# Attention scores on 32-row tiles of TensorE, four tiles at a time, in a transformer and state-space block on one Trainium2 core

## The chip, the cores and the metric

The kernel runs on one core of a Trainium2 chip. The metric is the device time of one execution in microseconds. TensorE multiplies matrices (PE in the profile, its weight loads PEld), VectorE is DVE, ScalarE is ACT, GpSimd is POOL, and SyncE (SP) issues transfers.

## The reference

Two layers work on x of shape (4, 256, 512). Layer 0 adds an attention and a gated feed-forward network, both of the normalized x; layer 1 adds a selective scan and a mixture of experts. What matters here is layer 0's attention:

```python
C_q = x @ Wq_d + bq_d                                   # 12 numbers per token
C_kv = x @ Wkv_d + bkv_d                                # 4 numbers per token
q = (C_q @ W_qk + b_qk).reshape(b, s, 32, 4)            # 32 heads of 4
scores = jnp.einsum('bqhd,bkd->bhqk', q, C_kv) / jnp.sqrt(4)
attn = jax.nn.softmax(scores, axis=-1)
V = (C_kv @ Wv_u + bv_u).reshape(b, s, 32, 16)
out = jnp.einsum('bhqk,bkhd->bqhd', attn, V).reshape(b, s, 512)
return out @ Wo + bo
```

All heads share the keys C_kv, and a head's contraction has length 4. The feed-forward network runs beside it: `silu(x @ W_gate.T) * (x @ W_up.T) @ W_down.T` with an inner width of 1792.

## The kernel before, in words

The order of the work is written out by hand (`tc.manual_schedule()`); each engine executes its instructions in the order of the program text. Layer 0 takes batches 0 and 1 as a first half and batches 2 and 3 as a second.

**Latents.** `latents(b)` (L269) makes the queries and keys of batch b, as a generator whose steps are put between other work. An fp32 value is held as two fp32r parts, high and low, each in four rows of a group of eight (for keys: two high copies, one low part and ones). `pkm` (L289) multiplies the keys `ks` with the selection `selk`; there are four selections, one for each position h4 = 0..3 of a head in its group of four, and each leaves the rows of the other three heads at zero. The result `km` has 128 rows and four versions, of 256 keys each. The queries `qg` have 128 rows too: 4 heads of 32 rows, for 4 groups gq and 2 halves hf, so 32 heads.

**Maxima.** `scores_max(b, j)` (L324) makes scores with queries on the partitions: for one gq, hf and query block qb, two matmuls (L329) of all 128 rows of `qg` with two versions of `km` each, 512 columns, into one PSUM tile `sc` of 1024 columns; zeros in `km` pick the head. VectorE then reduces it to four maxima (L331). Sixteen calls make a batch. `put_max(b)` (L336) transposes the maxima and adds them into rows of `qg` with eight VectorE instructions (L348), so that the next product is already score minus maximum.

**Attention.** `attention(b, ff, after, first, step, side)` (L467) runs eight steps k, one for each pair of key block c and head position h4. In each, `attend(b, k, t)` for t = 0, 1 makes transposed scores (keys on the partitions) with two matmuls `scT` (L361) of 128 rows, 512 columns, and ScalarE takes exp of 1024 columns (L363) into `pe`. `weigh(b, k-1)` (L365) sums the values `zk` with the weights of the step before: four matmuls of 32 output columns each, on four column tiles (fp32, so eight passes, L371). If `after` holds, which is so for b = 0 and 2, each step also has two calls of `scores_max` for batch b+1, one on each side of `weigh`. The maxima of batches 0 and 2 are made ahead, each in a loop of its own (L525, L552), together with `second`, the latents of the next batch. `normalize` (L375) copies the sums, multiplies them with a matrix that repeats the denominators (`pden`, L380), and VectorE divides.

`sc` and `scT` share the pool `pssc`, which has two slots of two PSUM banks. Other matmul results go to `psmm`, three slots of one bank.

**Feed-forward beside it.** `ff` is a generator: `gate_up(th)` (L403) makes, for 14 chunks, a gate (`pg`) and an up product (`pu`) of eight matmuls each of 512 columns (L417), and yields after every two; ScalarE takes tanh, VectorE multiplies (L425, L427), ScalarE rounds (L428), GpSimd makes the low part (L429) and issues the loads of weights `wgu` three products ahead. That is 112 pieces for each half. `go(ff, n)` runs n of them. `step` says how many pieces a step of attention takes, and `first` how many run behind `put_max`. After the first half, `down(0, i)` is the generator in place of `gate_up`.

After layer 0, pools are closed and layer 1 starts: projections, then a scan of 128 steps on VectorE (L909), with decays on ScalarE (L888), products on GpSimd (L913) and sums on TensorE (L925).

Of the kernel before, what the change touches and what calls it, by code (L numbers as in the profile page):

```python
# [17 lines left out]
P = 128  # L18
B, S, D = 4, 256, 512
# [22 lines left out]
def block_kernel(  # L42
# [24 lines left out]
    nc = tc.nc  # L67
    mm = nc.tensor.matmul
# [15 lines left out]
    ident = cst[:, C_ID : C_ID + P]  # L84
# [8 lines left out]
    psmm = ctx.enter_context(tc.tile_pool(name="psmm", bufs=3, space=PSUM))  # L93
# [8 lines left out]
    ap1 = att.enter_context(tc.tile_pool(name="att", bufs=1, side="right"))  # L102
# [18 lines left out]
    make = fold.enter_context(tc.tile_pool(name="fold", bufs=1))  # L121
# [4 lines left out]
    zq = make.tile([P, 4, 4 + P], F32, name="zq")  # L126
    nc.gpsimd.memset(zq, 0.0)

    zs = make.tile([40, 4, P], F32, name="zs")
    nc.gpsimd.memset(zs, 0.0)  # L130
    zz = make.tile([40, S], F32, name="zz")
    nc.gpsimd.memset(zz, 0.0)
    selq = ap1.tile([P, 4, 4 + P], F32R, name="selq")
    selk = ap1.tile([40, 4, P], F32R, name="selk")
    ks = ap1.tile([40, S], F32R, name="ks")
    mask = ap1.tile([P, 8], F32, name="mask")

# [9 lines left out]
    def selections():  # L147
        zh = zq[:, :, 4:].rearrange("p g (h r) -> p g h r", h=4)
        for r in (0, 8):
            nc.gpsimd.tensor_copy(zh[:, :, :, r : r + 4], idh[:, :, :, 0:4])  # L150
        nc.gpsimd.tensor_copy(selq, zq)
        for h4 in range(4):
            for k in range(2):
                nc.gpsimd.tensor_copy(
                    zs[32 * k : 32 * k + 8, h4, 32 * h4 + 8 * k : 32 * h4 + 8 * k + 8].rearrange(
                        "p (a r) -> p a r", a=2
                    ),
                    ident[32 * k : 32 * k + 8, 32 * k : 32 * k + 4].unsqueeze(1)
                    .to_broadcast([8, 2, 4]),
                )  # L160
            nc.gpsimd.tensor_copy(
                zs[0:8, h4, 32 * h4 + 16 : 32 * h4 + 24], ident[0:8, 4:5].to_broadcast([8, 8])
            )
        nc.gpsimd.tensor_copy(selk, zs)
        nc.gpsimd.tensor_copy(ks, zz)
# [101 lines left out]
    qs, kms = {}, {}  # L267

    def latents(b):  # L269
# [12 lines left out]
        yield  # L282
        yield

        km = ap1.tile([P, 4, S], F32R, tag="km", name="km", bufs=2)
        for h in range(2):
            p = psmm.tile([P, 2, S], F32, tag="mm", name="pkm")
            for i in range(2):
                mm(p[:, i, :], lhsT=selk[:, 2 * h + i, :], rhs=ks, start=True, stop=True)  # L289
            (nc.scalar.copy if h else nc.vector.tensor_copy)(km[:, 2 * h : 2 * h + 2, :], p)  # L290
        kms[b] = km
        yield
        pq = psmm.tile([P, 2, S], F32, tag="mm", name="pq")
        q8 = ap1.tile([P, 2, S], F32, tag="q8", name="q8")
        for hf in range(2):
            mm(pq[:, hf, :], lhsT=wqk[:, 1 + hf * P : 1 + (hf + 1) * P], rhs=cq,
               start=True, stop=True)
# [17 lines left out]
        for gq in range(4):  # L315
            p = psmm.tile([P, 2, S], F32, tag="mm", name="pqg")
# [4 lines left out]
            (nc.scalar.copy if gq % 2 else nc.vector.tensor_copy)(qg[:, gq], p)  # L321
            yield

    def scores_max(b, j):  # L324

        gq, hf, qb = j // 4, j // 2 % 2, j % 2
        sc = pssc.tile([P, 2, 512], F32, tag="sc", name="sc")
        for hp in range(2):
            mm(sc[:, hp, :], lhsT=qs[b][:, gq, hf, qb * P : (qb + 1) * P],  # L329
               rhs=kms[b][:, 2 * hp : 2 * hp + 2, :], start=True, stop=True)  # L330
        nc.vector.tensor_reduce(  # L331
            mpl2[b % 2][:, qb, :, 16 + 2 * gq + hf].rearrange("p (a i) -> p a i", a=2),
            sc.rearrange("p a (i k) -> p a i k", i=2), AX.X, ALU.max,
        )

    def put_max(b):  # L336
# [15 lines left out]
    avs, pes = {}, {}  # L352

    def attend(b, k, t):

        c, h4 = k // 4, k % 4
        if t == 0:
            pes[b, k] = ap1.tile([P, 4, 512], F32, tag="pe", name="pe", bufs=2)
        sc = pssc.tile([P, 2, 512], F32, tag="sc", name="scT")
        for j in range(2):  # L360
            mm(sc[:, j, :], lhsT=kms[b][:, h4, c * P : (c + 1) * P], rhs=qs[b][:, 2 * t + j],  # L361
               start=True, stop=True)
        nc.scalar.activation(pes[b, k][:, 2 * t : 2 * t + 2, :], sc, AF.Exp)  # L363

    def weigh(b, k):  # L365

        c, h4 = k // 4, k % 4
        if k == 0:
            avs[b] = psav.tile([P, 2, S], F32, tag="av", name="av")
        for gq in range(4):  # L370
            mm(avs[b][32 * gq : 32 * gq + 32].rearrange("p a b -> p (a b)"),  # L371
               lhsT=zk[:, 2 * b + c, 24 - 8 * h4 : 56 - 8 * h4], rhs=pes[b, k][:, gq, :],
               start=(c == 0 and h4 == 0), stop=(c == 1 and h4 == 3))

    def normalize(b, ff):  # L375
# [80 lines left out]
    def go(gen, n=1000):  # L456
        for _ in range(n):
            if next(gen, 1) == 1:
                break
# [7 lines left out]
    def attention(b, ff, after, first, step, side=()):  # L467

        put_max(b)
        go(ff, first)  # L470
        side = list(side)
        for k in range(8):
            attend(b, k, 0)
            go(ff, 1)
            attend(b, k, 1)
            go(ff, 1)
            if after:
                scores_max(b + 1, 2 * k)
            if k:
                weigh(b, k - 1)  # L480
            if after:
                scores_max(b + 1, 2 * k + 1)
            go(ff, step - 2)
            if side:
                f, *args = side.pop(0)
                f(*args)
        go(ff, 1)
        weigh(b, 7)
        go(ff, 1)
        normalize(b, ff)  # L490
# [28 lines left out]
    ff = gate_up(0)  # L519
    masks()  # L520
    first, second = latents(0), latents(1)
    for _ in range(9):
        go(first, 1)
        go(ff, 1)
    for j in range(16):  # L525
        scores_max(0, j)
        if j in (4, 8):
            fold_att(j // 8)
            go(ff, 1)
        else:  # L530
            go(ff, 2 if j % 3 else 1)
        if j % 2 == 1:
            go(second, 1)
    go(second)
    attention(0, ff, True, 8, 4)
    attention(1, ff, False, 8, 2, [(ln_begin, 1)] + [(ln_stats, 1, i) for i in range(4)]
              + [(ln_root, 1, 0, 4), (ln_scale, 1, 0, 2)])
    go(ff)
# [10 lines left out]
    for _ in range(9):  # L549
        go(first, 1)  # L550
        go(ff, 1)
    for j in range(16):  # L552
        scores_max(2, j)
        go(ff, 2)
        if j % 2 == 1:
            go(second, 1)
    go(second)
    go(ff)
    hidden(1)
    ff = gate_up(1)  # L560
    attention(2, ff, True, 10, 4)
# [700 lines left out]
    for u in range(total + 2):  # L1262
# [8 lines left out]
        if last >= 0 and last % NU == NU - 1:  # L1271
            c = last % PER // NU
# [124 lines left out]
```

## Time and profile before

| what | value |
|---|---|
| median of three runs | 887.26 us (887.15 to 890.01) |
| the profiled execution's own time | 889.37 us |
| its span, first to last instruction | 887.6 us |
| mean granted clock of TensorE | 0.927 |
| TensorE, VectorE, ScalarE, GpSimd busy | 85%, 77%, 59%, 55% |
| maxima of batch 0 | 29.0 to 60.3 us |
| attention of batches 0 and 1 | 60.3 to 110.3 and 110.3 to 148 us |
| maxima of batch 2 | 177.4 to 211 us |
| attention of batches 2 and 3 | 211 to 261.5 and 261.5 to 307 us |
| all after that | 307 to 888 us |

The stages are cut where `put_max` and `normalize` of a batch stand in the trace. A matmul of 512 columns has a duration of about 0.39 us in the records, while the next one starts 0.23 us after it: the records include the time to flow through, so prices are taken from differences of starts. fp32 matmuls count as two passes. A busy share of TensorE therefore says whether something is in flight, not how well it is used.

### The profile page before, as it was taken

What the parts mean: (1) busy time and instruction counts of PE and PEld (TensorE: products, weight loads), DVE (VectorE), ACT (ScalarE), POOL (GpSimd) and SP (SyncE); (2) the same over time, 40 slices, a digit from 0 to 9 for tenths busy, and PEclk for the clock granted to TensorE, in tenths of its full rate; (3) what the DMA queues carried; (4) which work ended last, traced back from release to release, by engine and by line L of the source; (5) the groups of instructions that cost most, each with busy time, mean ns of one, the idle gap of its engine ahead of it and who ended that gap; (6) DMA issues with size and microseconds to landing.
All of it is one profiled execution on the core that took longest, in us unless ns stands there. A gap on an engine that the chain in (4) does not pass through costs nothing.

```text
span 887.6 us, 10460 instructions
## 1 busy us (share of the span) xinstructions
PE 756.4 (85%) x3554; PEld 434.2 (49%) x3554; DVE 685.2 (77%) x675; ACT 525.8 (59%) x1009; POOL 489.9 (55%) x377
## 2 busy tenths in 40 slices
PE   5999989999989999998687898668898777965966
PEld 3675555667556576665453444334454433422422
DVE  4695554377565333878999999999999999999995
ACT  4225445312536437678787687776786794855561
POOL 4222222001223242758967789869689759697664
PEclk9999999899999999978997999888999889989896
DMA  6232242001112231374741645341646232426200
GB/s 213 60 95 72 72 119 71 13 1 36 48 48 72 72 116 26 96 185 153 239 111 51 165 120 159 98 127 54 166 134 163 84 96 75 126 72 178 72 24 24
DMA packets 67343, 86.67 MB, mean 98 GB/s; under 512 B 12077, under 2 KB 52025, under 8 KB 66906
## 3 DMA queue, kind: packets, MB, share of 16 engines
q1 hardware_dynamic: 57930, 67.12, 27.0%
q0 software_dynamic: 9072, 18.35, 7.5%
q8 instruction: 28, 0.46, 0.2%
q10 hardware_dynamic: 288, 0.52, 0.2%
q14 instruction: 25, 0.20, 0.1%
HBM read 66.58 MB, written 10.22 MB: 87 GB/s over the span
## 4 chain that ended last, share of the span: by engine, by line
DVE 39%; PE 36%; ACT 11%; POOL 6%; issue 5%; DMA 2%; SPq 0%; DVEq 0%; ACTq 0%; POOLq 0%
DVE h L909 23%; DVE bx L894 8%; ACT decay L888 5%; PE pu L417 5%; PE pg L417 4%; POOL hc L913 4%; PE sc L329 4%; PE av L371 3%; PE po L442 3%; PE scT L361 3%; PE px L696 2%; PE po L1017 2%; ACT pe L363 1%; PE ysum L925 1%; PE pqg L319 1%
## 5 line engine op out<-in xcount | busy, mean ns | idle before, releaser
L913 POOL TENSOR_TENSOR hc<-h,cr 128x1024 f32<-128x1024 f32 (+1 forms) x131 | 301.9, 2307 | 100.6 <-DVE h L909 89.1
L909 DVE TENSOR_TENSOR_SCAN h<-decay,bx 128x1024 f32<-128x1024 f32 (+1 forms) x129 | 288.0, 2234 | 15.6 <-PE po L442 3.9
L888 ACT ACTIVATE decay<-dts,aneg 128x255 f32<-128x255 f32 x504 | 213.6, 498 | 121.0 <-DVE h L909 110.6
L925 PE MATMUL ysum<-hc,stack 128*32 128x256 f32 x1024 | 93.0, 432 | 83.8 <-POOL hc L913 83.6
L894 DVE TENSOR_TENSOR bx<-brow,dus 128x1024 f32<-128x1024 f32 x128 | 157.6, 1231 | 3.7
L429 POOL TENSOR_TENSOR hlo<-g,hhi 128x512 fp32r<-128x512 f32 x28 | 36.1, 1290 | 148.5 <-ACT hhi L428 148.5
L331 DVE TENSOR_REDUCE mpl<-sc 128x4 f32<-128x1024 f32 x64 | 77.2, 1222 | 24.1 <-PE sc L329 23.8
L925 PEld LDWEIGHTS ysum<-hc,stack 128*32 128x32 f32 x1024 | 21.8, 113 | 146.0 <-POOL hc L913 125.5
L400 POOL DMA_DIRECT2D wgu<-in_wgu x56 | 31.2, 557 | 92.7 <-PE pg L417 82.4
L363 ACT ACTIVATE pe<-scT 128x1024 f32<-128x1024 f32 x64 | 62.7, 1023 | 29.9 <-PE scT L361 29.6
L1017 PE MATMUL po<-ow,xc 128*128 128x512 f32 x128 | 73.2, 682 | 2.2 <-DVE xc L929 2.2
L857 PE MATMUL pz<-xn1T,w_in 128*128 128x256 f32 x256 | 67.0, 409 | 0.0
L696 PE MATMUL px<-xn1T,w_in 128*128 128x256 f32 x256 | 64.7, 401 | 0.7 <-DMA w_in<-in_inx 0.6
L696 PEld LDWEIGHTS px<-xn1T,w_in 128*128 128x128 f32 x256 | 51.0, 202 | 20.4 <-issue 11.1
L425 DVE SCALAR_TENSOR_TENSOR g<-g,pg 128x512 f32<-128x512 f32 x28 | 19.2, 685 | 52.0 <-ACT g L424 52.0
L857 PEld LDWEIGHTS pz<-xn1T,w_in 128*128 128x128 f32 x256 | 48.8, 200 | 18.6 <-issue 11.7
L428 ACT CAST hhi<-g 128x512 fp32r<-128x512 f32 x28 | 17.4, 620 | 61.5 <-DVE g L427 61.2
L417 PE MATMUL pg<-xhi,wgu 128*128 128x512 f32 x112 | 47.1, 421 | 5.4 <-issue 2.9
L417 PE MATMUL pu<-xhi,wgu 128*128 128x512 f32 x112 | 47.8, 427 | 1.5 <-DVE g L427 0.7
L442 PE MATMUL po<-wd,hhi 128*128 128x512 f32 x112 | 49.0, 437 | 0.0
L329 PE MATMUL sc<-km,qg 128*128 128x512 f32 x128 | 43.9, 424 | 3.3 <-ACT pe L363 2.8
L417 PE MATMUL pg<-xlo,wgu 128*128 128x512 f32 x112 | 45.7, 408 | 0.0
(225 smaller groups left out, 1256.8 us busy)
## 6 DMA issues: line engine op xcount, KB each, us to landing
dts<-dtd SPq DMA_DIRECT2D x124, 128.0 KB, 2.9
dus<-dud SPq DMA_DIRECT2D x124, 128.0 KB, 2.9
wgu<-in_wgu POOLq DMA_DIRECT2D x56, 256.0 KB, 2.7
w_in<-in_inz SPq DMA_DIRECT2D x16, 512.0 KB, 4.7
w_in<-in_inx SPq DMA_DIRECT2D x15, 512.0 KB, 4.6
dtd<-dt SPq DMA_DIRECT2D x15, 256.0 KB, 2.2
dud<-du SPq DMA_DIRECT2D x15, 256.0 KB, 2.3
wd<-in_wd POOLq DMA_DIRECT2D x7, 512.0 KB, 3.6
```

Of the source, the lines that this page charges most:

```text
L329: mm(sc[:, hp, :], lhsT=qs[b][:, gq, hf, qb * P : (qb + 1) * P], rhs=kms[b][:, 2 * hp : 2 * hp + 2, :], start=True, stop=True)
L331: nc.vector.tensor_reduce(mpl2[b % 2][:, qb, :, 16 + 2 * gq + hf].rearrange("p (a i) -> p a i", a=2), sc.rearrange("p a (i k) -> p a i k", ...
L417: mm(ps, lhsT=wgus[i][:, hc, :], rhs=xs[j][:, hc, :], start=(hc == 0 and j == 0), stop=(hc == HC - 1 and j == 1))
L442: mm(po, lhsT=hids[th][j][:, m, i * P : (i + 1) * P], rhs=wd[:, m, :], start=False, stop=(m == MC - 1 and j == 1))
L696: mm(px[:, i, :], lhsT=w[:, i, hc, :], rhs=xns[b][:, hc, :], start=(hc == 0), stop=(hc == HC - 1))
L857: mm(pz[:, i, :], lhsT=w[:, i, hc, :], rhs=xns[b][:, hc, :], start=(hc == 0), stop=(hc == HC - 1))
L888: nc.scalar.activation(da[:, k, 1:], live["dts", b, c][:, k, 1:], AF.Exp, scale=aneg[:, c, k, g : g + 1])
L894: nc.vector.tensor_tensor(bx, brow[g // 2][:, g % 2, :].unsqueeze(1).to_broadcast([P, NG, S]), live["dus", b, c], ALU.mult)
L909: nc.vector.tensor_tensor_scan(h[:, n].rearrange("p n t -> p (n t)"), da[:, n].rearrange("p n t -> p (n t)"), bx[:, n].rearrange("p n t -> ...
L913: nc.gpsimd.tensor_tensor(hc[:, n], h[:, n], crows[b][:, g, :].unsqueeze(1).to_broadcast([P, NG // parts, S]), ALU.mult,)
L925: mm(ysum[k * NB : (k + 1) * NB, :], lhsT=stack, rhs=hc[:, k, :], start=False, stop=(g == NU - 1))
L1017: mm(live["po", b, i], lhsT=xcs[b][:, c, i * P : (i + 1) * P], rhs=late_w["ow"][:, c, :], start=False, stop=(c == DC - 1))
```

## The change

The keys' product is made once for all heads: `selk` has all four head positions in its columns, and `km` has 256 columns in place of 4 x 256, with the rows of each head position filled.

The scores of a head position then come from its 32 rows alone: matmuls of 32 rows at partitions 0, 32, 64 or 96. `attend` takes for its groups gq the positions gq ^ h4, so that the two matmuls of a call lie on two different row tiles, 0 and 1 or 2 and 3; `weigh` takes the values accordingly. `scores_max(b, k, hp)` makes, for one gq and qb, the two halves hf of two head positions 2hp and 2hp+1: four matmuls of 256 columns, on two row tiles. In `attention` it is called right behind each `attend`, with the pair of positions that `attend` does not use. The sums (`weigh`) stand right behind the second of them. In batches 1 and 3 the two calls of `attend` stand together, with the sums right behind. The two loops for batches 0 and 2 make both pairs of positions one after the other. The pieces of feed-forward between are dealt out anew; `step` is 5 instead of 4 for batches 0 and 2.

```diff
-    zs = make.tile([40, 4, P], F32, name="zs")
+    zs = make.tile([40, P], F32, name="zs")
...
-    selk = ap1.tile([40, 4, P], F32R, name="selk")
+    selk = ap1.tile([40, P], F32R, name="selk")
...
-        km = ap1.tile([P, 4, S], F32R, tag="km", name="km", bufs=2)
-        for h in range(2):
-            p = psmm.tile([P, 2, S], F32, tag="mm", name="pkm")
-            for i in range(2):
-                mm(p[:, i, :], lhsT=selk[:, 2 * h + i, :], rhs=ks, start=True, stop=True)
-            (nc.scalar.copy if h else nc.vector.tensor_copy)(km[:, 2 * h : 2 * h + 2, :], p)
-        kms[b] = km
+        kms[b] = ap1.tile([P, S], F32R, tag="km", name="km", bufs=2)
+        p = psmm.tile([P, S], F32, tag="mm", name="pkm")
+        mm(p, lhsT=selk, rhs=ks, start=True, stop=True)
+        nc.scalar.copy(kms[b], p)
...
-    def scores_max(b, j):
+    def rows(h):
+        return slice(32 * h, 32 * h + 32)
 
-        gq, hf, qb = j // 4, j // 2 % 2, j % 2
+    def scores_max(b, k, hp):
+
+        gq, qb = k // 2, k % 2
         sc = pssc.tile([P, 2, 512], F32, tag="sc", name="sc")
-        for hp in range(2):
-            mm(sc[:, hp, :], lhsT=qs[b][:, gq, hf, qb * P : (qb + 1) * P],
-               rhs=kms[b][:, 2 * hp : 2 * hp + 2, :], start=True, stop=True)
+        for hf in range(2):
+            for i in range(2):
+                w = rows(2 * hp + i)
+                mm(sc[:, i, hf * S : (hf + 1) * S], lhsT=qs[b][w, gq, hf, qb * P : (qb + 1) * P],
+                   rhs=kms[b][w], start=True, stop=True)
         nc.vector.tensor_reduce(
-            mpl2[b % 2][:, qb, :, 16 + 2 * gq + hf].rearrange("p (a i) -> p a i", a=2),
-            sc.rearrange("p a (i k) -> p a i k", i=2), AX.X, ALU.max,
+            mpl2[b % 2][:, qb, 2 * hp : 2 * hp + 2, 16 + 2 * gq : 18 + 2 * gq],
+            sc.rearrange("p i (f k) -> p i f k", f=2), AX.X, ALU.max,
         )
...
         for j in range(2):
-            mm(sc[:, j, :], lhsT=kms[b][:, h4, c * P : (c + 1) * P], rhs=qs[b][:, 2 * t + j],
+            gq = 2 * t + j
+            w = rows(gq ^ h4)
+            mm(sc[:, j, :], lhsT=kms[b][w, c * P : (c + 1) * P], rhs=qs[b][w, gq],
                start=True, stop=True)
...
         for gq in range(4):
+            h = gq ^ h4
             mm(avs[b][32 * gq : 32 * gq + 32].rearrange("p a b -> p (a b)"),
-               lhsT=zk[:, 2 * b + c, 24 - 8 * h4 : 56 - 8 * h4], rhs=pes[b, k][:, gq, :],
+               lhsT=zk[:, 2 * b + c, 24 - 8 * h : 56 - 8 * h], rhs=pes[b, k][:, gq, :],
...
         for k in range(8):
-            attend(b, k, 0)
-            go(ff, 1)
-            attend(b, k, 1)
-            go(ff, 1)
-            if after:
-                scores_max(b + 1, 2 * k)
+            for t in range(2):
+                attend(b, k, t)
+                if after:
+                    scores_max(b + 1, k, 1 - (t ^ k // 2 % 2))
+                    if t == 0:
+                        go(ff, step - step // 2)
             if k:
                 weigh(b, k - 1)
-            if after:
-                scores_max(b + 1, 2 * k + 1)
-            go(ff, step - 2)
+            go(ff, step // 2 if after else step)
...
-    for j in range(16):
-        scores_max(0, j)
-        if j in (4, 8):
-            fold_att(j // 8)
-            go(ff, 1)
-        else:
-            go(ff, 2 if j % 3 else 1)
-        if j % 2 == 1:
-            go(second, 1)
+    for k in range(8):
+        scores_max(0, k, 0)
+        scores_max(0, k, 1)
+        if k in (2, 4):
+            fold_att(k // 4)
+        go(ff, 3)
+        go(second, 1)
     go(second)
-    attention(0, ff, True, 8, 4)
+    attention(0, ff, True, 8, 5)
```

The loop for batch 2 changes in the same way (four pieces behind each pair of calls), and so does `attention(2, ff, True, 10, 4)` to a step of 5.

More of the change, by code (lines that the diff above doesn't have):

```diff
@@ L154, in selections @@
                 nc.gpsimd.tensor_copy(
-                    zs[32 * k : 32 * k + 8, h4, 32 * h4 + 8 * k : 32 * h4 + 8 * k + 8].rearrange(
+                    zs[32 * k : 32 * k + 8, 32 * h4 + 8 * k : 32 * h4 + 8 * k + 8].rearrange(
                         "p (a r) -> p a r", a=2
@@ L161, in selections @@
             nc.gpsimd.tensor_copy(
-                zs[0:8, h4, 32 * h4 + 16 : 32 * h4 + 24], ident[0:8, 4:5].to_broadcast([8, 8])
+                zs[0:8, 32 * h4 + 16 : 32 * h4 + 24], ident[0:8, 4:5].to_broadcast([8, 8])
             )
@@ L551, in block_kernel @@
         go(ff, 1)
[L552 to L556, printed above, removed]
+    for k in range(8):
+        scores_max(2, k, 0)
+        scores_max(2, k, 1)
+        go(ff, 4)
+        go(second, 1)
     go(second)
@@ L560, in block_kernel @@
     ff = gate_up(1)
-    attention(2, ff, True, 10, 4)
+    attention(2, ff, True, 10, 5)
     attention(3, ff, False, 10, 4, [(pre_stats, 0), (pre_stats, 1), (pre_scale,), (pre_turn, 0),
```

## The prediction

> **What bounds the kernel now.** I read the slices of the page first, then the chain of waits by line, then the busy times by stage, and last the timeline of one step of the changed loop.
>
> ```profile
> PE   5999989999989999998687898668898777965966
> DVE  4695554377565333878999999999999999999995
> ...
> DVE 39%; PE 36%; ACT 11%; POOL 6%; issue 5%; DMA 2%; SPq 0%; DVEq 0%; ACTq 0%; POOLq 0%
> ```
>
> One slice is 22.2 us. In slices 1 to 14 (22 to 333 us) TensorE stands at 8 and 9 and VectorE at 3 to 7, but for a 9 in slice 2 (44 to 67 us, the maxima of batch 0); after that VectorE takes over with the scan, which the change does not touch. So the first 318 us are a TensorE stage. The chain by line gives the scores 4% (L329) and 3% (L361), some 57 us together, and the weighted sums (L371) 3%. By stage (the three rows are attention of batches 0, 1 and 2; in brackets the number of instructions):
>
> ```profile
> core 0: us, PE busy (x) PEld busy (x) DVE busy (x) ACT busy (x) POOL busy (x), PEclk, DMA share, GB/s
> ...
> 60.30:110.30 50.00, 47.18 (x221) 29.03 (x222) 29.16 (x36) 22.32 (x28) 13.58 (x19) 1.00 0.27 74
> 110.30:148.00 37.70, 33.49 (x157) 18.12 (x156) 16.97 (x31) 22.64 (x27) 9.17 (x14) 0.95 0.30 84
> ...
> 211.00:261.50 50.50, 49.47 (x227) 29.47 (x225) 29.76 (x36) 22.59 (x28) 12.26 (x16) 1.00 0.21 56
> ```
>
> TensorE is busy 89 to 98% of them, VectorE and ScalarE 45 to 60%. One step k of attention(0), on TensorE (start, duration, both us; "x2" is two matmuls merged):
>
> ```profile
> 69.42 0.62 PE L361 MATMUL scT<-qg,km 128*128 128x512 f32 x2
> 69.88 0.39 PE L417 MATMUL pu<-xhi,wgu 128*128 128x512 f32 x1
> 70.11 0.40 PE L417 MATMUL pu<-xlo,wgu 128*128 128x512 f32 x1
> 70.34 0.62 PE L361 MATMUL scT<-qg,km 128*128 128x512 f32 x2
> 70.80 0.40 PE L417 MATMUL pu<-xhi,wgu 128*128 128x512 f32 x1
> 71.03 0.40 PE L417 MATMUL pu<-xlo,wgu 128*128 128x512 f32 x1
> 71.27 0.62 PE L329 MATMUL sc<-km,qg 128*128 128x512 f32 x2
> 71.83 1.06 PE L371 MATMUL av<-pe,zk 128*32 128x512 f32 x8
> 72.82 0.73 PE L329 MATMUL sc<-km,qg 128*128 128x512 f32 x2
> 73.39 0.39 PE L417 MATMUL pu<-xhi,wgu 128*128 128x512 f32 x1
> ```
>
> The prices are differences of starts. A score matmul takes (69.88-69.42)/2 = 0.23 us. The second one of the pair at 71.27 has streamed at 71.73; the column-tiled sums start at 71.83: **0.10 us to change the array's shape**. The eight passes of the sums take 0.99 us with the way out (0.90 of streaming, 0.09 of draining), where eight full matmuls would take 1.84: four column tiles do run at once. The pair after them needs 73.39-72.82 = 0.57 instead of 0.46: **0.11 us of weight load that nothing hides** after a change of shape. A step has 8 score and 8 other matmuls (16 x 0.23 = 3.68) and the sums (0.10+0.99+0.11 = 1.20): 4.88 us. The starts of the steps give (101.84-64.64)/7 = 5.31 in batch 0 and (251.99-215.87)/7 = 5.16 in batch 2, so 0.43 and 0.28 of each step are waits; the list of waits has TensorE at L329 waiting for ScalarE's exp (L363) five times, 2.7 us.
>
> **What the Trainium skill says.** "TensorE: Matmul & The Clock Gate", Part 3 (Packing small matmuls — row/col tiling): matmuls on different 32-row strips run together; four with K=32, N=512 were measured at 3.07 times. A weight load overlaps matmuls in flight when its row group differs. The trace of before has no two row tiles; its column tiles agree in kind. The same page, LDWEIGHTS: a load takes its columns divided by 1.2 GHz (107 ns for 128), whatever its rows. The trace agrees: 0.11 above, and here four loads of 40 rows in 0.53 us, the last taking 0.19 with its latency, so one every (0.53-0.19)/3 = 0.11:
>
> ```profile
> 18.56 0.53 PEld L289 LDWEIGHTS pkm<-ks,selk 40*128 40x128 f32 x4 [0.87 <-issue]
> ```
>
> "TensorEngine Tiling (Array Packing)", Key Properties: changing the tiling mode drains the engine; that is the 0.10 and 0.09. Its Gotcha 1: different row tiles may not write one PSUM bank at once. The change gives each row tile its own 512-column half of sc or scT.
>
> **The change part by part.** All is summed against the profiled execution, 889.37 us.
>
> 1. *Attention 0 and 2, two score groups a step.* Before, a group's share is two scT and two sc matmuls, 4 x 0.23 = 0.92. After, it is six matmuls on four row tiles. If they run at once: drain 0.10, load 0.11, streaming 0.24, drain 0.09, load of the next full matmul 0.11, together 0.65, 0.27 less. The second group has the sums right behind, whose own entry (0.10) and exit are in the 1.20 already: 0.10+0.11+0.24 = 0.45, 0.47 less. So 0.74 a step, x16 = **-11.8**.
> 2. *Attention 1 and 3, one group a step.* Four matmuls on four row tiles and the sums behind: 0.45 for 0.92; x16 = **-7.5**.
> 3. *Maxima of batches 0 and 2 alone, eight groups each.* Eight matmuls of 256 columns, two on each tile. Taken in order, the second pair of heads starts one half-length (0.11) late: 0.10+0.11+0.35+0.09+0.11 = 0.76 for 0.92; x16 = **-2.6**. VectorE's 9 in slice 2 could keep batch 0's half of it (1.3).
> 4. *Keys' product once.* One matmul for four at 0.117, in four batches: **-1.4**. VectorE loses four copies of 0.69, ScalarE's four shrink; both lie beside TensorE: 0. On GpSimd the memset of zs (0.52) and the copy to selk (0.60) shrink ahead of the first wgu loads; these are issued by 11.6 us and needed at 16.9: 0.
> 5. *More feed-forward in a step (5 for 4).* It moves work between stages that TensorE bounds: 0, while there is enough left. The first half has 112 pieces; 9 beside the latents, 24 beside the maxima, 54 in attention 0 (8 ahead, 8 x 5, 6 behind) and 25 in attention 1 use them up before its last sums, so none is left for the second normalize, which had three. Its ScalarE copy (0.58) and the landing of the sums (0.17) then keep pden, and all that is queued behind it on TensorE, waiting: **+0.9**.
> 6. *New waits.* In attention 1 both exps of a step (2 x 1.02) must end before the next group has both of its slots: 0.11+0.24+0.17 to the result, 2.04, 0.1 to signal, 2.66, and a share of tanh and cast; I take 2.75. TensorE's own step is 2.56 (four ff matmuls 0.92, group 0.45, sums 1.19): 0.2 x 8 = **+1.5**. Attention 3 has 3.48 and is not held. In attention 0 and 2 I leave the waits at 0.43 and 0.28: the maximum (1.22) behind a gate multiply (0.69) reaches 2.5 us after a group's start, while the next group comes after 2.0 and 2.6. They could vanish (-5.7) or double (+5.7).
>
> DMA: wgu loads come with 15% more haste in those steps, still three tiles (over 4 us) ahead of a landing of 2.7 us: 0. Nothing is moved on SP's queue. GpSimd's order of hlo and loads is kept.
>
> Sum: -11.8-7.5-2.6-1.4+0.9+1.5 = **-20.9**, 868.5 for the profiled execution. That execution stands 2.1 above the median of 887.26, so 866.4: I say 867, with 859 to 873 from the waits.
>
> **The rivals.**
>
> *Weight loads one after another.* It rests on the 0.11 above: if loads into different row strips do not overlap, a group is as long as its loads. Six: 0.10+0.66+0.11+0.09+0.11 = 1.07 for 0.92 alone and 0.87 before the sums, +0.10 a step, +1.6. Four: 0.10+0.44+0.23 = 0.77, -2.4. Eight: 0.10+0.88+0.11+0.09+0.11 = 1.29, +5.9. With -1.4 and +0.9: +4.6, **892, slower**. It decides once a lone group of six takes over about 0.9 us. For it: no two 128-column loads in this trace are closer than 0.11. Against: four loads for column tiles start within 0.02 of each other, and a measured 3.07 leaves no room for loads in a row.
>
> *The two score slots become the bound.* Each group takes both pssc slots, and each half-step of attention 0 and 2 is paced by 0.5 to the result, 0.69+1.22 on VectorE, 0.1 to signal, 2.6 with the drain: 5.2 a step against 5.77 and 5.62 (before plus one more ff piece), 8 us in all; attention 1 gains nothing, attention 3 keeps 3.8, the maxima alone fall to 1, as VectorE with 26.1 of 31.3 us is near: about 12, **875**. For it: the exp and maximum waits already there. Against: VectorE at 60%.
>
> *It does not do what it says.* Row tiles that exclude each other altogether, loads too: six take 2 x 0.34 + 4 x 0.22 = 1.56, eight 1.76; +26 or so, **905 and more**. The column tiles speak against it.
>
> **How the numbers follow.** At once: 0.60. Slots: 0.16. Loads in a row: 0.18, two fifths of it near no change, since the four-groups and a shorter wait can pay for the rest. Excluding: 0.06. A measurement tells 0.3% (2.7 us) from no change. Faster 0.76, same 0.07, slower 0.17. The range 859 to 889 holds the first two and a third of the third case.
>
> **What would show it.** In the changed trace: the first four matmuls of an attention group starting within 0.05 us, with loads as close (right) or 0.11 apart (the first rival); a group alone at 0.65; the first step period of attention 1 near 2.75; the start of the scan's stage some 20 us earlier with an unchanged length; a gap of 0.9 ahead of the second pden. Wrong would be a stage after 318 us that changes by more than 2 us, or a TensorE that waits for L363 and L335 longer than before.

## The result and the profile after

The changed kernel took 876.07 us (median of four runs, 874.84 to 880.3) beside 888.24 for the kernel before: a ratio of 0.987, 95% interval 0.9831 to 0.9908. It was run again, unedited, in two of the later comparisons: 871.87 us, ratio 0.9802 [0.9753, 0.985], and 876.83 us, ratio 0.9816 [0.9768, 0.9864]. All three intervals lie below 1: faster, by 1.3 to 2.0%. An execution more than 1.5% above the fastest of its kernel is left out of the ratios; in what follows that is one of the six of a later variant, the early root (879.84 us). The forecast was 867 us, a ratio of 0.977, with 859 to 873 from the waits. So the direction and most of the size came (12, 17 and 14 us of the 20 forecast), but two of the three medians lie above that narrower range. The first profiled execution of the changed kernel (880.3 us, span 878.5) is the slowest of its four runs; that of the first repeat (871.22, span 869.4) is close to its median, so times by stage are taken from the repeat, against a repeat of the kernel before (889.3, span 887.5).

The slices and the chain by engine, changed kernel, first profiled execution; one slice is 22 us:

```profile
PE   5899988999989999986877997777998778966965
...
DVE  4587653477663435779899999999999999999995
...
PEclk9899988999999999978789899789999878988997
...
PE 42%; DVE 31%; ACT 12%; POOL 7%; issue 5%; DMA 2%; SPq 0%; DVEq 0%; ACTq 0%; POOLq 0%
```

The slices look as before: a gain of this size is less than one of them, so the page alone can't place it. TensorE still stands at 8 and 9 up to slice 14 and VectorE, but for one 8, at 9 through the scan. What has changed is PEclk, with an 8 in slice 1 (22 to 44 us, in the maxima of batch 0) and in slices 5 and 6 (110 to 154 us, the attention of batch 1), where the kernel before had 9; its own 8 of that part stands in slice 7. The chain's shares are no evidence: they are 42 and 31% for TensorE and VectorE here, 31 and 39% in the repeat.

One attention group and the full matmuls around it on TensorE, then the group's weight loads, same execution (start, duration, both us; "x4" is four merged):

```profile
67.78 0.39 PE L424 MATMUL pg<-xlo,wgu 128*128 128x512 f32 x1
68.10 0.49 PE L367 MATMUL scT<-qg,km 32*128 32x512 f32 x2
68.11 0.50 PE L333 MATMUL sc<-km,qg 32*128 32x256 f32 x4
68.54 0.50 PE L424 MATMUL pg<-xhi,wgu 128*128 128x512 f32 x1
68.88 0.40 PE L424 MATMUL pg<-xlo,wgu 128*128 128x512 f32 x1
```

```profile
68.10 0.18 PEld L367 LDWEIGHTS scT<-qg,km 32*128 32x128 f32 x2 [0.36 <-issue]
68.11 0.30 PEld L333 LDWEIGHTS sc<-km,qg 32*128 32x128 f32 x4
```

The first four matmuls and their four weight loads start within 0.01 us, on four row tiles; the last two `sc` follow on tiles that are already in use. Between the two full matmuls at 67.78 and 68.54 lie 0.76 us, of which 0.23 is the first one's own streaming: 0.09 to drain and 0.44 for the group. The matmul at 68.88 starts 0.34 behind its neighbour instead of 0.23: 0.11 of load that nothing hides. 0.09 + 0.44 + 0.11 = **0.64 us for what took 0.92**.

Two stages of the repeat, attention of batches 0 and 1 (columns as in the prediction), and behind them the second of these in the repeat of the kernel before:

```profile
60.70:107.90 47.20, 46.55 (x274) 26.46 (x273) 31.03 (x38) 24.64 (x32) 18.01 (x24) 1.00 0.38 109
107.90:143.90 36.00, 29.87 (x149) 13.81 (x147) 16.09 (x30) 22.42 (x27) 8.53 (x12) 0.91 0.27 78
```

```profile
112.60:150.10 37.50, 31.77 (x158) 17.40 (x157) 16.11 (x30) 22.68 (x27) 9.03 (x12) 1.00 0.29 82
```

Batch 0 is at full clock with TensorE busy 99% of the time, and batch 2 likewise (47.6 of 48.1 us). In batch 1 it is busy 83%, at a clock of 0.91; the kernel before stands at 85% and 1.00 there. In this stage the gain was lost.

The same comparison by stage, in us, repeat minus repeat. A feed-forward piece is two matmuls, 0.46; the third column takes out the pieces that the change moved from one stage to another. The boundary of a stage can be set some 0.2 us earlier or later.

| stage | difference | for the same work | forecast |
|---|---|---|---|
| to the end of the maxima of batch 0 | -0.55 | -0.55 | -2.0 |
| attention 0 (8 pieces more) | -4.17 | -7.9 | -5.9 |
| attention 1, to the second pden (4 fewer) | -1.44 | +0.4 | -1.35 |
| down and maxima of batch 2 (4 fewer) | -3.03 | -1.2 | -2.0 |
| attention 2 (8 more) | -3.34 | -7.0 | -5.9 |
| attention 3, to its pden | -2.73 | -2.7 | -3.75 |
| to the first scan (8 fewer) | -4.22 | -0.5 | 0 |
| all ahead of the first scan | -19.48 | -19.5 | -20.9 |

The half-clock stretches described below fall into other stages in other executions. In the third execution of the changed kernel, where attention 1 and the stage behind it have one such stretch each instead of two, the same rows give -0.9 and -1.8 for the same work, and all ahead of the scan -23.0. In the first, attention 1 gives +2.7, and all ahead of the scan, against the first execution of the kernel before, -13.7. The rows of attention 0, 2 and 3 agree within 0.1 us in all three.

The first scan starts at 342.3 instead of 361.7 us. From it to the end it takes 527.2 beside 525.8. The first profiles had shown 531.3 beside 526.7 there, and the third of the changed kernel shows 529.9. Over all fourteen profiles of this study the stage lies between 524.7 and 531.3, in no order of the edits, so whether the 0.5 to 5.5 us by which the changed kernel's three profiles exceed the two of the kernel before belong to the change stays open.

### The profile page after: what moved, and what is told of

It is laid out like the page before. It is cut to its first block, busy times and chain, and to the rows that moved or that the text cites. A ratio compares the mean times of both kernels' runs of the same rounds, so it can differ in the third digit from the quotient of the medians.

```text
span 878.5 us, 10684 instructions
## 1 busy us (share of the span) xinstructions
PE 746.8 (85%) x3670; PEld 412.1 (47%) x3670; DVE 682.2 (78%) x671; ACT 525.9 (60%) x1009; POOL 489.2 (56%) x377
## 4 chain that ended last, share of the span: by engine, by line
PE 42%; DVE 31%; ACT 12%; POOL 7%; issue 5%; DMA 2%; SPq 0%; DVEq 0%; ACTq 0%; POOLq 0%
DVE h L912 17%; DVE bx L897 6%; PE pg L424 5%; ACT decay L891 5%; PE po L449 5%; POOL hc L916 5%; PE pu L424 4%; PE av L378 3%; PE pz L860 3%; PE pp L743 2%; PE ysum L928 2%; PE po L1020 2%; DVE mpl L335 2%; PE px L699 2%; PE scT L367 2%
## 5 line engine op out<-in xcount | busy, mean ns | idle before, releaser
L860 PE MATMUL pz<-xn1T,w_in 128*128 128x256 f32 x256 | 69.1, 418 | 0.0
L860 PEld LDWEIGHTS pz<-xn1T,w_in 128*128 128x128 f32 x256 | 49.6, 203 | 19.5 <-issue 12.2
L424 PE MATMUL pg<-xhi,wgu 128*128 128x512 f32 x112 | 50.7, 453 | 5.4 <-issue 2.9
L435 ACT CAST hhi<-g 128x512 fp32r<-128x512 f32 x28 | 17.3, 620 | 59.6 <-DVE g L434 59.6
L424 PE MATMUL pu<-xhi,wgu 128*128 128x512 f32 x112 | 51.3, 458 | 0.7 <-DVE g L434 0.7
L424 PE MATMUL pu<-xlo,wgu 128*128 128x512 f32 x112 | 46.2, 413 | 0.0
```

What stands on the lines that cost most here:

```text
L424: mm(ps, lhsT=wgus[i][:, hc, :], rhs=xs[j][:, hc, :], start=(hc == 0 and j == 0), stop=(hc == HC - 1 and j == 1))
L860: mm(pz[:, i, :], lhsT=w[:, i, hc, :], rhs=xns[b][:, hc, :], start=(hc == 0), stop=(hc == HC - 1))
```

## The experiments

### The unedited kernels again

> A second look at the kernel before, nothing edited, for the spread of the granted clock. Theory 1: first scan near 361 us with 8 to 12 us of clock lost ahead of it, and 527 us from there to the end. Rival (chance): first scan to end anywhere from 526 to 532 us.

> A second look at the changed kernel, nothing edited. Theory 1 (the scores save what was forecast, 20 us, and half-rate stretches of the TensorE clock[...] take part of it back): 873 to 880 us; what the clock loses ahead of the first scan differs from 15.4 us by some 3.4 us steps, and the first scan starts earlier or later than 347.2 us by the same amount; the stretch from the first scan to the end stays near 531 us if the loss there is caused by the change. Rival (the longer scan stage is chance): first scan to end 527 us, as before.

> The changed kernel once more, unedited, on the same chip as the three versions below: 871 to 877 us. Theory 1 (the changed kernel's own spread comes from half-rate stretches of the clock): whatever its profiled execution takes above or below 869.4 us of span is found, within 2 us, in clock lost ahead of the first scan and in the length of the scan stage. Rival (waits differ from run to run): the same lists of waits would show other lengths.

The times are above. What the three executions of the changed kernel teach is their spread: the scan started at 347.2, 342.3 and 338.7 us. The program is the same, but the trace's record of TensorE's granted clock is not. It falls to one half for stretches of 3.4 us or multiples of it. Ahead of the scan they cost 15.4, 10.2 and 3.4 us of clock (time multiplied by the share not granted), and between the first and the third about 0.7 us of each us lost shows in the start of the scan ((347.2 - 338.7)/(15.4 - 3.4)). That is a mean: the kernel before lost 8.5 and 6.8 and started its scan at 360.9 and 361.7. One such stretch, first execution, maxima of batch 0:

```profile
36.27 0.50 PE L333 MATMUL sc<-km,qg 32*128 32x256 f32 x4 [0.66 <-DVE mpl L335]
37.40 0.50 PE L333 MATMUL sc<-km,qg 32*128 32x256 f32 x4 [0.63 <-DVE mpl L335]
...
43.67 0.63 PE L424 MATMUL pg<-xhi,wgu 128*128 128x512 f32 x1
44.10 0.63 PE L424 MATMUL pg<-xlo,wgu 128*128 128x512 f32 x1
```

TensorE waits twice for VectorE's maximum; soon after (38.8 to 45.6) full matmuls follow each other at 0.43 us instead of 0.23. This one stands behind such idling, and so does the one at 141 us in attention 1, but similar waits in the other executions were not always followed by one: in the third, attention 1 has the same late step (4.23 us) and no such stretch behind it. What decides it stays open.

### The order alone, with full matmuls

The kernel before, with the changed kernel's order of calls, its pairs in the maxima loops and its step of 5 in attention 0 and 2; every score matmul keeps its 128 rows.

```diff
-            attend(b, k, 0)
-            go(ff, 1)
-            attend(b, k, 1)
-            go(ff, 1)
-            if after:
-                scores_max(b + 1, 2 * k)
+            for t in range(2):
+                attend(b, k, t)
+                if after:
+                    scores_max(b + 1, 2 * k + t)
+                    if t == 0:
+                        go(ff, step - step // 2)
             if k:
                 weigh(b, k - 1)
-            if after:
-                scores_max(b + 1, 2 * k + 1)
-            go(ff, step - 2)
+            go(ff, step // 2 if after else step)
...
```

> The kernel before with full 128-row score matmuls and its four key products, but in the new order: maxima right behind each transposed pair, sums right behind, pieces of feed-forward dealt out as in the change (step 5). If the gain is concurrency alone: no less TensorE work, the uncovered second normalize costs 0.9, so 886 to 892 us. If the order itself gives part of the gain: 878 to 884.

Measured: 885.8 us (20 runs), ratio 0.9959 [0.9939, 0.998], between the two forecasts. TensorE's waits for a score slot up to the scan (us in total, times, longest), first in the repeat of the kernel before (5.4 us together), then here (2.3):

```profile
PE sc L329 <- ACT pe L363: 2.8, 6, 0.7
PE scT L361 <- ACT pe L363: 1.3, 3, 0.6
PE scT L361 <- DVE mpl L331: 0.8, 1, 0.8
PE sc L329 <- DVE mpl L331: 0.5, 2, 0.3
```

```profile
PE sc L329 <- DVE mpl L331: 1.3, 4, 0.4
PE scT L361 <- ACT pe L363: 1.0, 3, 0.7
```

A step takes 5.30 us in batch 0 and 5.26 in batch 2, with five pieces. TensorE's own work for that is 4.88 + 0.46 = 5.34 in a step with sums; but step 0 has no sums (`if k`), so the seven differences between eight starts hold six of them, and the mean share is 5.34 - 1.20/7 = 5.17. What waits is 0.13 and 0.09 a step. Counted in the same way, where 4.88 - 1.20/7 = 4.71 are TensorE's own, the kernel before waits 5.31 - 4.71 = 0.60 and 5.16 - 4.71 = 0.45, and not 0.43 and 0.28. So the order takes away most of the waits that the prediction left in place. The whole of this edit is worth 0.4%. Which part of the new order does it (I take it to be the pieces on both sides of each pair of calls, which leave a slot longer to be read out) was not tried.

### The row tiles alone, in the old order

The changed kernel's row tiles and keys, with its calls back where the kernel before has them: the two pairs of `attend` apart from each other, one call of `scores_max` on each side of `weigh`, the maxima loops in single calls, steps of 4.

```diff
-            for t in range(2):
-                attend(b, k, t)
-                if after:
-                    scores_max(b + 1, k, 1 - (t ^ k // 2 % 2))
-                    if t == 0:
-                        go(ff, step - step // 2)
+            attend(b, k, 0)
+            go(ff, 1)
+            attend(b, k, 1)
+            go(ff, 1)
+            if after:
+                scores_max(b + 1, k, 0)
             if k:
                 weigh(b, k - 1)
-            go(ff, step // 2 if after else step)
+            if after:
+                scores_max(b + 1, k, 1)
+            go(ff, step - 2)
...
```

> The changed kernel's row tiles and single keys' product, but in the order of before: a piece of feed-forward between the two transposed pairs, sums between the two maxima, the maxima alone taken one call at a time, step 4. Theory 1 (each change of the array's shape costs a drain and a bare weight load, so row tiles pay only where four stand together): a lone pair takes 0.10+0.11+0.23+0.09+0.11 = 0.64 us against 0.46 of two full matmuls; +0.36 us in each of 32 steps, +0.18 in each of 32 lone maxima, -1.4 for the keys: about +16 us on the kernel before, 895 to 908. Rival (concurrency of pairs pays by itself): 878 to 886.

Measured: 898.02 us (20 runs), ratio 1.007 [1.0047, 1.0093]: slower than before, as the first theory had it. A lone pair in this kernel, on TensorE:

```profile
75.75 0.40 PE L424 MATMUL pg<-xlo,wgu 128*128 128x512 f32 x1
76.08 0.50 PE L367 MATMUL scT<-qg,km 32*128 32x512 f32 x2
76.51 0.50 PE L424 MATMUL pg<-xhi,wgu 128*128 128x512 f32 x1
76.85 0.40 PE L424 MATMUL pg<-xlo,wgu 128*128 128x512 f32 x1
```

From 75.75 to 76.85 are 1.10 us, less 0.46 for two full matmuls: 0.64 for a pair that takes 0.46 on all rows, and the same 0.64 that the changed kernel pays for six. A group on row tiles costs its two changes of shape, whether two matmuls stand in it or six, as long as no tile streams more than 512 columns. The old order has four groups in a step of attention 0, two at 0.64 and two, next to the sums, at 0.43: 2.14 for the 1.84 of eight full matmuls, so 4.88 - 1.84 + 2.14 = 5.18 a step of TensorE's own, 5.01 in the mean over seven; 5.22 is measured. The changed kernel has two groups, 0.64 + 0.44 = 1.08. The steady steps of attention 1 go from 3.05 to 3.18 us, those of attention 3 from 3.94 to 4.26 on average.

So order alone gives 0.9959, tiles alone 1.007, and both together 0.9802, each against the kernel before on its own chip. **Nearly all of the gain is the two together**: the order is what lets the tiles pay.

### Neighbouring matmuls on one row tile

The changed kernel, but with the two `scT` of a call on the same row tile; the values in `weigh` follow.

```diff
-            w = rows(gq ^ h4)
+            w = rows(h4)
...
-            h = gq ^ h4
+            h = h4
```

> The changed kernel, but both transposed score matmuls of a call lie on the same row tile (heads at the same position in both groups), so only the maxima's matmuls can run beside them. If the gain is concurrency of row tiles: a pair takes 0.46 us instead of 0.24 and shares a tile with half of the maxima, +0.67 us a step in 16 steps and +0.69 in 16 steps, about +20 us where TensorE bounds: 890 to 898 us. If the gain came from the new order and the single keys' product: within 4 us of the changed kernel, 872 to 880.

Measured: 887.91 us (20 runs), ratio 0.9954 [0.9927, 0.998], 1.8% over the changed kernel's 871.87 and slightly below my theory's 890. A group alone, between feed-forward matmuls, on TensorE:

```profile
82.25 0.49 PE L367 MATMUL scT<-qg,km 32*128 32x512 f32 x1
82.26 0.50 PE L333 MATMUL sc<-km,qg 32*128 32x256 f32 x4
82.59 0.39 PE L367 MATMUL scT<-qg,km 32*128 32x512 f32 x1
82.91 0.50 PE L424 MATMUL pg<-xhi,wgu 128*128 128x512 f32 x1
```

Its two `scT`, now on one tile, start 0.34 apart (82.25, 82.59) and no longer together, while the `sc` on other tiles still start with the first of them. The group takes 82.91 - 82.25 = 0.66 us for 0.44. In the step's second group, where two of the four `sc` share that tile as well, it is 0.89 for 0.44 (84.49 to the sums at 85.38):

```profile
84.49 0.49 PE L367 MATMUL scT<-qg,km 32*128 32x512 f32 x1
...
85.38 1.06 PE L378 MATMUL av<-pe,zk 128*32 128x512 f32 x8
```

That is 0.67 a step; the steps of attention 0 from 82.25 on take 5.26, beside 4.71 for the same steps of the changed kernel. Attention 1's take 3.25 for 2.58. Number, rows and order of the matmuls are the same, only the tiles differ: the gain is different row strips running at once, not shorter contractions. Its size is less sure than its cause: up to the scan this profiled execution is 19.1 us behind the repeat of the changed kernel, of which the four attention stages give 12.3; another 7.2 lie in the maxima loop of batch 0, which the edit leaves as it was, and where 17 us stand at half clock.

### Where attention 1 lost its gain

Its steps run at 2.56 to 2.59 us, below the 2.75 of the forecast, but the last one does not. Repeat of the changed kernel, TensorE and then ScalarE:

```profile
134.73 0.40 PE L424 MATMUL pu<-xlo,wgu 128*128 128x512 f32 x1
136.44 0.50 PE L367 MATMUL scT<-qg,km 32*128 32x512 f32 x2 [1.31 <-ACT pe L369]
137.35 0.50 PE L367 MATMUL scT<-qg,km 32*128 32x512 f32 x2 [0.42 <-ACT pe L369]
```

```profile
132.46 1.28 ACT L209 ACT_TABLE_LOAD   x1
133.75 0.30 ACT L209 ACTIVATE rs<-mv,eps 128x4 f32<-128x4 f32 x1
134.07 1.28 ACT L369 ACT_TABLE_LOAD   x1
135.36 1.94 ACT L369 ACTIVATE pe<-scT 128x1024 f32<-128x1024 f32 x2
```

`attention` also takes a list of small side steps, one behind each k; here the last two are the normalization of the second half of x. Its square root (L209) needs another function table, so ScalarE loads one, takes the root of 128x4 numbers and loads the first one again: 2.9 us between two exps. The next group waits 1.31 + 0.42 for them, and then the clock falls to one half: from 139 to 142 us full matmuls follow each other at 0.43 again. The variants that follow act on this.

First, **the root behind the last exp**: root and scale are moved to k = 7. Second, **one piece less a step** in attention 0, which leaves pieces over for the second normalize. Third, **both**.

```diff
+    def ln_behind():
+        ln_root(1, 0, 4)
+        ln_scale(1, 0, 2)
...
-              + [(ln_root, 1, 0, 4), (ln_scale, 1, 0, 2)])
+              + [(go, ff, 0), (go, ff, 0), (ln_behind,)])
```

```diff
-    attention(0, ff, True, 8, 5)
+    attention(0, ff, True, 8, 4)
```

> The changed kernel, but in attention 1 the square root of the next half's layer normalization, with its two table loads (1.28 us each on ScalarE), stands behind the last exp of the batch instead of between the exps of steps 5 and 6. If those loads are what takes back the gain of attention 1: step 6 to 7 falls from 4.24 to 2.6 us, the wait of TensorE for the exp (1.31 us) goes, and with it the half-rate stretch behind it: 3 us less than the changed kernel, 868 to 872. If they are covered anyway: no difference beyond 1 us.

> The changed kernel with a step of 4 instead of 5 pieces in attention 0 only, so that eight pieces of feed-forward are left behind attention 1. If the uncovered copy ahead of pden (0.9 us) and the idle end of attention 1 cost what was forecast: 1 to 2 us less than the changed kernel. If the two score slots bound attention 0 (rival): its step stays near 4.7 us in place of 4.2 and the moved pieces cost 3 to 4 us more in the whole.

> Both edits: square root behind the last exp, and a step of 4 in attention 0. If the two losses of attention 1 are separate: 3 to 5 us less than the changed kernel, 866 to 870. If one covers the other: as the better of the two.

Measured: 875.51 (ratio 0.9837 [0.9798, 0.9875]), 872.48 (0.9795 [0.976, 0.983]) and 872.71 us (0.98 [0.9757, 0.9842]), six runs each: none differs measurably from the changed kernel's 0.9802 and 0.9816 (measured on other chips). So none of the gains that were forecast shows. One piece less a step shows how near the two score slots are to being the limit: TensorE's own work falls by 0.46 a step, but the steps of attention 0 fall only from 4.69 to 4.53 us in the mean over seven, so most of the room goes into waits. The late root is a miss that teaches something. Its last steps take 2.56 to 2.84, but (TensorE's wait, then ScalarE, then VectorE):

```profile
PE pden L387 <- ACT o L384: 3.1, 1, 3.1
```

```profile
141.30 0.62 ACT L435 CAST hhi<-g 128x512 fp32r<-128x512 f32 x1 [1.87 <-DVE g L434]
141.82 0.58 ACT L384 COPY o<-av 128x512 f32<-128x512 f32 x1
```

```profile
139.46 0.17 DVE L213 RECIPROCAL rs<-rs 128x2 f32<-128x2 f32 x1 [3.17 <-ACT rs L209]
...
140.58 0.68 DVE L434 SCALAR_TENSOR_TENSOR g<-g,pu 128x512 f32<-128x512 f32 x1
```

Read it by its waits: the copy of the sums (L384) stands behind a rounding (L435), that waits for VectorE's multiply (L434), that stands behind a reciprocal and two scalings, and these wait for the root (L209), which ended at 139.4 behind its table load. The delay went from the scores to `pden`, along three engines' queues.

**The root early.** In this variant the statistics are taken in attention 0's side list and the root, with the reload of the exp table, right behind attention 0; the same for layer 1's first normalization, behind attention 2. The scalings stay where they were. Only the lines for attention 0 and 1 are shown. It was also run with a step of 4 in attention 0 (second text below), and with that and one piece more behind each of the first five pairs in the maxima loop of batch 0 (third).

```diff
-    attention(0, ff, True, 8, 5)
-    attention(1, ff, False, 8, 2, [(ln_begin, 1)] + [(ln_stats, 1, i) for i in range(4)]
-              + [(ln_root, 1, 0, 4), (ln_scale, 1, 0, 2)])
+    attention(0, ff, True, 8, 5, [(ln_small, 1)] + [(ln_stats, 1, i) for i in range(4)])
+    ln_root(1, 0, 4)
+    nc.scalar.preload_act_table_set("exp_and_others")
+    attention(1, ff, False, 8, 2, [(ln_begin, 1)] + [(go, ff, 0)] * 5 + [(ln_scale, 1, 0, 2)])
...
```

> The changed kernel, but the square roots of both layer normalizations that lie beside attention 1 and 3 are taken, with their table loads, between attention 0 and 1 and between 2 and 3, where ScalarE is idle for 9 and 4 us; their statistics move to VectorE in attention 0 and 2. If table loads between exps take back the gain of attention 1 (1.3 us of wait, 1.7 of half rate) and 1.3 us in attention 3: both stages keep steps of 2.6 and 3.5 us without a long one, 3 to 4 us less than the changed kernel. If 3.5 us more of statistics hold the maxima in attention 0: its step rises above 4.7 and the gain is gone.

> The same with a step of 4 in attention 0, so that eight pieces of feed-forward cover the last sums and the second normalize of the first half: 1 us less than v_early, if the 0.9 us wait of pden is the only bare one left.

> The same as v_early_cover with five of those pieces put beside the maxima of batch 0 (four instead of three behind each of the first five pairs), where TensorE waits 1.8 us for VectorE's maxima. If that stage is bound by VectorE (26.6 of 33.7 us busy): the pieces cost little there and the wait goes, 1 to 2 us less than v_early_cover. If TensorE bounds it: no difference.

Measured, beside the changed kernel's 0.9816 [0.9768, 0.9864] in the same comparison: 868.01 us (862.55 to 879.84), ratio 0.9725 [0.9682, 0.9768]; 872.59 us, 0.9798 [0.9754, 0.9841]; 868.43 us, 0.9746 [0.9708, 0.9784]. The end of attention 1 with the early root (lines are 11 further down in this kernel):

```profile
134.10 0.40 PE L435 MATMUL pu<-xlo,wgu 128*128 128x512 f32 x1
134.43 0.50 PE L378 MATMUL scT<-qg,km 32*128 32x512 f32 x4
```

The last group follows its neighbour at 0.33 instead of 1.71 us, and ahead of the scan TensorE's waits for the exps fall from 2.5 to 0.7 us. Attention 1 takes 32.1 us (107.33 to 139.43) beside 34.65 for the changed kernel in the same comparison, attention 0 takes 48.4 beside 47.2. That rise lies in its steps, 4.86 for 4.69 in the mean, where VectorE now takes the statistics beside the maxima, as the second expectation had it; two steps of 5.3 and 5.6 make it. Up to the scan the profiled executions differ by 2.7 us in all; the other 5.2 of the 7.9 us between their spans fall in the scan's stage, which this edit does not touch, so the medians' difference of 8.8 us is more than the edit is shown to give. Its interval just touches that of the changed kernel. Of what ran, the early root has the lowest median, with its third form 0.4 us behind; that it beats the kernel before is measured, that it beats the changed kernel is likely and not more, since with a step of 4 beside it the ratio is back at 0.9798. Pieces kept as cover for `pden`, which still waits 0.9 with the early root, brought nothing that can be measured here. The five pieces put beside the maxima of batch 0 lengthen that stage by 1.5 us (61.7 beside 60.2, with as much clock lost) for 2.3 us of their own, so they fill waits there only in part.

## Why the prediction was right, and where its terms were off

**The mechanism holds.** Row tiles run at once, their loads too: starts within 0.01 us, a group alone at 0.64 (0.65 forecast), a group ahead of the sums at 0.44 (0.45). That four tiles run at once, and that the order is needed for it to pay, are shown by experiments; what the single keys' product gives was not run by itself. What rested on "TensorE: Matmul & The Clock Gate" of the Trainium skill, Part 3, is shown here by one edit that keeps every matmul and changes only its tile. The rival of loads in a row would have given 1.07 and a slower kernel; that of tiles that exclude each other 1.56. Both fall with the first lines of the trace. The price that the prediction took from the column tiles' change of shape (0.10 in, 0.09 out, 0.11 of bare load) carried over to row tiles unchanged.

**The sum is near, its terms less so.** In the repeats it is -19.5 of -20.9 before the scan. That it comes so near is in part luck: item 1 is 3.1 better than forecast, items 2 to 4 together 5.0 worse, and the other executions give -13.7 and -23.0.

1. *Attention 0 and 2, -14.9 for -11.8.* The step "I leave the waits at 0.43 and 0.28" failed twice. The waits were larger, 0.60 and 0.45, because the mean over seven steps holds six sums and not seven. And they shrank: the changed kernel's steps take 4.69 and 4.71, of which 4.60 - 0.17 = 4.43 are TensorE's own, so 0.26 and 0.28 are left. The order alone leaves still less (0.13 and 0.09), with longer steps. The prediction had "could vanish" within its range, and took the middle without asking which slot each group would find free.
2. *Attention 1, +0.4 for -1.35.* The term "2.75 for the step" was too high (2.58 measured) and the stage still lost: the named limit (two exps a step) did not bind, while a term that was not in the sum did, 2.9 us of table loads and root between two exps. In the kernel before, with its step of 3.07, no wait for an exp was longer than 0.7; a shorter step takes away cover also from what is not moved. The other part of the loss is clock: the repeat lost 3.4 us of it in this stage and the kernel before none. With 1.7 lost, in the third execution, the stage gives -0.9 for the same work; with 6.8, in the first, +2.7.
3. *Maxima alone, with keys, -1.75 for -4.0.* "VectorE's 9 in slice 2 could keep batch 0's half" was right in part: VectorE is busy 26.6 of 33.7 us, TensorE waits 1.8 us for its maxima (0.2 before), and 0.55 is what came; but five more pieces in that loop still cost 1.5 us of their 2.3, so TensorE's work counts there too. A group of eight cost less than forecast: 0.64 instead of 0.76 where both slots were free (first execution, from the full matmul at 29.29 to the second one behind the group at 30.39, less 0.46). What batch 2's loop lacks (-1.2 of -2.0) is mostly clock: it gives -1.8 in the third execution, which lost as much clock there as the kernel before.
4. *Attention 3, -2.7 for -3.75.* One step of 4.75 among steps of 3.5 to 3.9, again with a root between exps; it falls to 3.93 with the early root.
5. *The uncovered `pden`, 0.9 us:* measured 0.7 and 0.9.
6. *Not in the sum: the clock.* Between 3.4 and 15.4 us of TensorE's clock were lost ahead of the scan in three executions of one program. The clock granted over a whole execution is on record for all of them: on average 0.921 in the fourteen of the changed kernel; on the two chips where both kernels ran again, 0.924 beside 0.932 and 0.922 beside 0.929 for the kernel before. Among the fourteen, time goes with it, by 5.6 us for each 0.01 (correlation -0.83). If that slope holds between the kernels, 0.007 to 0.008 less clock is some 4 us, an estimate, of the 5 to 10 us by which the medians miss 867. That the change itself brings the lower clock is likely, since both chips show it, but no experiment changed the clock alone; why it would, stays open.

Of the signs that would have spoken against the forecast, both came in part. TensorE's waits for the score slots in the changed kernel, repeat, up to the scan:

```profile
PE sc L333 <- DVE mpl L335: 3.8, 6, 1.0
PE scT L367 <- ACT pe L369: 2.5, 4, 1.3
```

It waits less for the exps (2.5 us, 4.1 before) but more for the maxima (3.8 us, 1.3 before), together 6.3 for 5.4. The rival of the two slots was right about VectorE in the maxima loop. Its 5.2 a step for attention 0 and 2 was too much, but the 4.53 with one piece less shows that such a limit stands close below the changed kernel's 4.69. The other sign, a change of over 2 us after the start of the scan, stood in the first profile and in the third (529.9, at least 3.2 more than before), and not in the repeat; its cause stays open.

## What to carry to other kernels

Packing small matmuls into row tiles is paid per group, not per matmul: count how often the array changes shape, and pay for it (beyond its streaming, 0.40 us here for a group alone and 0.20 with another tiled operation right behind) only where enough matmuls stand together; by these prices a pair loses (0.64 for 0.46) and a group on all four tiles gains (0.64 for 0.92). When a step on the bounding engine is shortened, go through everything that the other engines do once in that step, such as a change of function table, since it may have been covered by the very time that is removed. Before changing the work of a loop, try its new order alone: here it was worth 0.4%, and without it the new work was a loss. When steps are averaged from their starts, count what each of them holds: here the first has no sums, and the waits came out too small by 0.17.

## What was not expected of the hardware

A lone pair of matmuls on two row tiles, a group of six on four and, with free slots, a group of eight of half the columns cost the same 0.64 us. TensorE's clock was granted at one half in stretches of 3.4 us and multiples, also after idling that came in pieces of 0.6 to 0.7 us, and executions of one program differ by up to 12 us of clock lost ahead of the scan. A root of 128x4 numbers between exps cost ScalarE 1.28 + 0.30 + 1.28 us, nine tenths of it for loading tables.
